# Choosing the buffers of attention probabilities in the kernel's own order account, and inverting layer 1's softmax sums in transposed form

## The chip, the cores and the metric

The kernel runs on one core of one Trainium2 chip. The metric is the device time of one execution in microseconds (us); the time before is the median of three runs. TensorE (PE) multiplies matrices into PSUM, VectorE (DVE) and ScalarE (ACT) work on SBUF and PSUM, GpSimd (POOL) does some elementwise work and issues the DMAs that accumulate, SyncE (SP) issues most others. In the profile PEld is PE's loading of weights, beside its matmuls.

## The reference, cut to what matters

Two layers on x of shape (8, 256, 32, 32), all in float32.

```python
# layer 0: convolutional attention, 8 heads of 32 channels, 1024 queries, 1426 pooled keys
x = x + L0(gn(x))
    # pooled(k_map), pooled(v_map): means at sides 32, 16, 11, 5, each plus a depthwise 3x3 of itself, then layernorm
    attn = softmax(einsum('bhqd,bhkd->bhqk', q_g, k) * SCALE)
    out  = proj(einsum('bhqk,bhkd->bhqd', attn, v) mixed by w_attn)
# layer 1: attention over the 1024 tokens of 256 channels, then 8 experts of three matrices each
t = tokens(x)
t = t + attention(layernorm(t))      # one head of 256
t = t + experts(layernorm(t))        # gate by softmax over the mean of the batch
```

Both softmaxes are computed without a maximum: exponentials, their sums, and a product with the reciprocal of the sum. A guard adds up sums and reciprocals of all softmaxes; should it find them too large, a general version runs behind a branch (it doesn't with these inputs).

## The kernel before, in words

Layer 0's attention is the spine of the first 1916 us. `steps` lists 8 images x 2 groups of four heads (c) x 2 halves of the queries x 11 chunks of 128 keys (the last 18 keys are done once per image, in `tail_scores`). In each step PE computes the scores of one chunk into the only sc buffer (4 PSUM banks, 128 x 2048), ACT takes their Exp into a tile pt (128 x 2048, 1 MB), and PE multiplies the previous step's pt with the values into pv. For the softmax sums, pt tiles are added in pairs: `add` lets an accumulating DMA on POOL's queue add the odd chunk's tile to the even one's; then, in `sums`, DVE adds the pairs 1 to 5 of a unit (b, c, half) to pair 0, and PE multiplies that with ones into a PSUM bank, total. There are six pt buffers. An odd tile is free when its values are multiplied and its DMA has landed, an even one after DVE's addition, that of pair 0 after the product with ones.

`normalise` turns total by 32 x 32 blocks on DVE (each sum stands 32 times, so 16 of 512 columns hold all), inverts 16 numbers, turns them back and multiplies. For the guard, ACT copies total and the reciprocals, 512 elements each, with an accumulator output into a column of `hi` and of `lo`.

Layer 1's attention runs beside it, an image or more behind: `layer1` computes scores and Exp (tiles p1, six buffers), `outputs` adds them up, multiplies with ones, inverts on DVE all 256 sums of a tile that stand in every partition, multiplies with the values and adds the residual. Its guard copies on ACT, of sums and reciprocals, stand before and after the reciprocal and write to the unused half of the same PSUM bank.

The order of every engine's instructions is fixed while the program is built. `Flow` (line 658) keeps an account: `now` for each engine, `ready` and `read` for each tile, with a cost for each operation (`cost`), and 0.15 us or a transfer time (`transfer`) until others see a result. Each piece of work is a generator that yields what it needs next; `step` resumes those that the account calls runnable, by rank, between the steps of the attention: the units have rank 0, layer 1 ranks 5 and 6, depthwise taps 7, expert tiles done ahead 8. `finish` resumes threads until a condition holds, and otherwise picks the one with the earliest start. `note` (line 766) books an instruction and ties it to the one before on its engine, so that every engine keeps the account's order; nearly all instructions are issued there, and so have line 671 in the profile.

`Flow.tile` (line 705) takes the buffer of the tag whose last tile ends first by the account, to book a start time. But which buffer a tile really gets is chosen by the tile framework among those of its tag, and the account doesn't know of uses of a tile that are not yet booked.

From about 1950 us on the experts run, three matrix products each for 8 experts and 16 tiles of 512 tokens, mostly as Strassen products with 7 instead of 8 partial products; a few tiles are done ahead during attention (`experts_ahead`, in the plain form).

Of the kernel before, what the change touches and what calls it, by code (L numbers as in the profile page):

```python
# [8 lines left out]
F32 = mybir.dt.float32  # L9
# [7 lines left out]
P = 128  # L17
C = 256
# [16 lines left out]
MARGIN = 1.5  # L35
AHEAD = {"DVE": 4.0, "ACT": 2.0, "POOL": 1.0, "SP": 10.0}
NEAR = {"DVE": 1.5, "ACT": 2.0, "POOL": 1.0, "SP": 10.0}
BUFS = {"sm": 2, "sx": 1}
AHEAD3 = 3
PACE2 = 8.0  # L40
# [13 lines left out]
class Kit:  # L54
# [3 lines left out]
        self.nc = nc  # L58
        self.n = 0

    def tile(self, pool, shape, tag, bufs=None):
        self.n += 1
        return pool.tile(shape, F32, tag=tag, name=f"{tag}_{self.n}", bufs=bufs)

    def rstd(self, out, var, eps):
# [592 lines left out]
class Flow:  # L658
# [27 lines left out]
    def __init__(self, tc, kit):  # L686
        nc = tc.nc
        self.tc, self.kit = tc, kit
        self.now = dict.fromkeys(("PE", "DVE", "ACT", "POOL", "SP"), 0.0)
        self.last = {}  # L690
        self.ready, self.read, self.writer, self.reader, self.slots, self.open = {}, {}, {}, {}, {}, set()
        self.pe = self.Engine(self, "PE", nc.tensor)
        self.ve = self.Engine(self, "DVE", nc.vector)
        self.act = self.Engine(self, "ACT", nc.scalar)
        self.pool = self.Engine(self, "POOL", nc.gpsimd)
        self.sp = self.Engine(self, "SP", nc.sync)
        self.threads = []
        self.cut = {}
        self.also = {}
        self.tiled = None  # L700
        self.columns = False
        self.left, self.served = [0.0, 0.0], 0.0
        self.credit, self.port = [0.0, 0.0], 0.0

    def tile(self, pool, shape, tag, bufs=1):
        t = self.kit.tile(pool, shape, tag, bufs=bufs)
        slots = self.slots.setdefault(tag, [None] * bufs)
        i = min(range(bufs), key=lambda i: self.end(slots[i]))
        self.ready[t.name] = self.end(slots[i])
        slots[i] = t.name  # L710
        if tag in BUFS:
            self.open.add(t.name)
        return t

    def end(self, name):

# [49 lines left out]
    def note(self, engine, op, ins, args, kwargs):  # L766
# [35 lines left out]
        if "dma" in op:  # L802
            both = out.space == DRAM and srcs[0].space == DRAM
            size = 4e-3 * out.shape[0] * out.free_size() if out.space != DRAM else 4e-3 * srcs[0].shape[0] * srcs[0].free_size()
            lag = self.transfer(engine, end, size * (0.0054 if engine == "POOL" or both else 0.003))
        for n in {*outs, self.key(out)}:
            self.ready[n] = max(self.ready.get(n, 0.0), end + lag)
            self.writer[n] = "DMA" if "dma" in op else engine
# [5 lines left out]
    def transfer(self, queue, at, work):  # L814

        span = max(0.0, at - self.served)
        self.served = max(self.served, at)
        mine, other = queue == "POOL", queue != "POOL"
        left = self.left
        both = 2 * min(left)  # L820
        done = min(span, both) / 2
        for i in range(2):
            left[i] = max(0.0, left[i] - done - max(0.0, span - both))
        left[mine] += work
        return 1.7 + left[mine] + min(left[mine], left[other]) + self.served - at

    @staticmethod
    def key(a):
# [85 lines left out]
def attention(tc, kit, f, outer, ended, nb, consts, x, t1, t2, hn, bounds, vecs, q_t, kv_t, proj_t, gqk_t, wqk, wqkv, vecs1, w1_d, w1c, gate_d, wrc, vecs2, bnvec, w2_d, h2d, between, pre, held):  # L914
# [6 lines left out]
    with ExitStack() as ctx:  # L921
# [39 lines left out]
        nc.scalar.dma_start(pjw, proj_t.rearrange("(k p) f -> p k f", p=P))  # L961
        con = kit.con
        ident, grp = kit.ident, con[:, K_GRP : K_GRP + P]
        heads = T(l1, [P, P + DH], "res", bufs=2)
        nc.scalar.dma_start(heads, consts[:, K_HEAD:K_SEL])
        head = heads[:, :P]
# [26 lines left out]
        def mix():  # L993
# [46 lines left out]
            yield act(wa)  # L1040
            f.act.activation(wa, wa, AF.Exp)
            yield ve(wa)
            rs = T(wp, [P, 2], "wars")
            f.ve.tensor_reduce(rs, wa, AX.X, ALU.add)
            f.ve.reciprocal(rs, rs)
# [18 lines left out]
            for c in range(2):  # L1064
                f.pe.matmul(
                    ps[:, c * C : (c + 1) * C], lhsT=bdt[:, c, :], rhs=pjw[:, c, :], start=True, stop=True
                )
            yield ve(ps)
            raw = T(l1, [P, 2, C], "s")
            f.ve.tensor_copy(raw, ps.rearrange("p (c q) -> p c q", c=2))  # L1070
            for c in range(2):
# [106 lines left out]
            return dy, dx, max(0, -dy), n - max(0, dy), max(0, -dx), n - max(0, dx)  # L1178


        pmaps = [T(pool_, [P, NK], f"p{i}") for i, pool_ in enumerate((between, work))]
        for t in pmaps:
            f.split(t, 512, HW)
        first, large, whole, pooled, asked, halved = {}, [], [], [], [], []
# [67 lines left out]
        def first_keys(half):  # L1252

            n = SIDES[0]
            middle, rest = first["diag"]
            for m in range(2):
                p, acc = first[m]
                pin = p[:, : n * n].rearrange("p (h w) -> p h w", h=n)
                yield pe(p[:, : n * n], middle, rest, tag="sm")
                ps = small()  # L1260
                pout = ps.rearrange("p (h w) -> p h w", w=n)
                for i, tap in enumerate((4, 0, 1, 2, 3, 5, 6, 7, 8)):
                    dy, dx, y0, y1, x0, x1 = windows(tap, n)
                    y0, y1 = max(y0, 16 * half), min(y1, 16 * half + 16)
                    f.pe.matmul(
                        pout[:, y0 - 16 * half : y1 - 16 * half, x0:x1],
                        lhsT=rest[:, 8 * m + i - 1, :] if i else middle[:, m, :],
                        rhs=pin[:, y0 + dy : y1 + dy, x0 + dx : x1 + dx],
                        start=i == 0,
                        stop=i == 8,  # L1270
                    )
                f.act.activation(acc[:, half * 512 : half * 512 + 512], ps, AF.Identity, bias=db(m, 0))
            large.append(("keys", half))

        def taps(c, s, p, acc, base=0):
# [324 lines left out]
        def sums(n, pairs):  # L1600

            for i in range(1, NKC // 2):
                yield until(lambda: len(pairs) > i)
                for j in range(0, 4, 2):
                    s = pairs[0][:, j : j + 2, :]
                    yield ve(s, pairs[i])
                    f.ve.tensor_tensor(s, s, pairs[i][:, j : j + 2, :], ALU.add)
            yield until(lambda: normalised[0] == n)
            yield pe(pairs[0], tag="sm")
            total = small()  # L1610
            for j in range(4):
                f.pe.matmul(
                    total[DH * j : DH * j + DH, :], lhsT=kit.ones[:, :DH], rhs=pairs[0][:, j, :], start=True, stop=True
                )
            return total

        def normalise(b, c, sl, total, n):
# [2 lines left out]
            turned = rec.rearrange("p (j i) -> p j i", i=DH)  # L1620
            yield ve(total)
            f.ve.transpose(rec, total)
            f.act.activation(total, total, AF.Copy, accum_out=hi[:, column[n] : column[n] + 1])
            one = T(work, [P, 16, 1], "one")
            f.ve.reciprocal(one, turned[:, :, 0:1])
            f.ve.transpose(turned, one.to_broadcast([P, 16, DH]))
            f.ve.tensor_tensor(att, att, rec, ALU.mult)
            yield act(rec)
            f.act.activation(rec, rec, AF.Copy, accum_out=lo[:, column[n] : column[n] + 1])

        def project(b):
            if b == nb - 1:
                last = T(work, [P, 2, HW], "pt", bufs=6)
                f.sp.dma_start(last, x[b].rearrange("(k p) n -> p k n", p=P))
            for m in range(2):
# [17 lines left out]
                        f.pool.dma_start(out=t1[b][:, m, sl], in_=xt, accum_op=ALU.add)  # L1653
            if b == nb - 1:
                f.sp.dma_start(t1[b], last)
            projected[0] += 1

        def scale_tokens(src, n):
# [90 lines left out]
        def outputs():  # L1749

            for i in range(4 * nb):
# [13 lines left out]
                ps = small()  # L1765
                f.pe.matmul(ps[:, :C], lhsT=kit.ones, rhs=s[:, 0, :], start=True, stop=True)
                yield ve(ps)
                rec = T(l1, [P, C], "rec1")
                n = 8 * (i // 4) + 4 + i % 4
                f.act.activation(ps[:, C:], ps[:, :C], AF.Copy, accum_out=hi[:, n : n + 1])  # L1770
                f.ve.reciprocal(rec, ps[:, :C])
                f.act.activation(ps[:, C:], rec, AF.Copy, accum_out=lo[:, n : n + 1])
                yield pe(*p1, v, tag="sm")
                ps = small()
                for m in range(2):
                    for kc in range(8):
# [7 lines left out]
                            stop=kc == 7,  # L1784
                        )
                taken[0] += 1
                yield ve(ps, rec)
                m2 = ps.rearrange("p (m q) -> p m q", m=2)
                f.ve.tensor_tensor(m2, m2, rec[:, None, :].to_broadcast([P, 2, C]), ALU.mult)
# [1 line left out]
                    f.ve.scalar_tensor_tensor(res[:, m, :], m2[:, m, :], gb[:, m : m + 1], res[:, m, :], ALU.add, ALU.add)  # L1791
                f.sp.dma_start(t2[b][:, :, q], res)
                f.spawn(norm(b, q, res), 5)

        scaled = [0]

# [24 lines left out]
        def weights1():  # L1821
# [76 lines left out]
            wrs = T(wp, [P, 2, NE], "wrs")  # L1898
            yield from centred(cm, wr, NE, wrs)
            f.sp.dma_start(wrc, wrs)  # L1900
            ready.append(True)

        gw, wv = (T(l1, [P, 2, C], tag) for tag in ("gw", "wv"))
# [4 lines left out]
        def experts_ahead():  # L1908

            yield until(lambda: made[0] == nb and key_parts[0] == 3 * nb)  # L1910
            for e, tag in enumerate(("p0", "kt")):
                w = held["w"][e] = T(between, [P, 2, 2, C], tag)
                f.sp.dma_start(w[:, 0], w1c[:, e])
                f.sp.dma_start(w[:, 1], w2_d[:, e])
# [48 lines left out]
        def unit(b, c, sl, n, pairs):  # L1963
            total = yield from sums(n, pairs)
            yield from normalise(b, c, sl, total, n)
            normalised[0] += 1
            if c and sl.start:
                f.spawn(project(b), 1)

        atts = {}  # L1970
        f.spawn(chain(*map(keys_and_values, range(nb))), 2)
# [21 lines left out]
        for i in range(len(steps) + 1):  # L1993
            if i < len(steps):
# [12 lines left out]
                if kc == NKC - 1:  # L2007
                    f.finish(lambda: key_parts[0] > 3 * b + 2 and (b, 1) in qs and (b or len(asked) == 4))
                    tail_scores(b)
                else:  # L2010
                    pts[i] = scores(b, c, sl, kc)
                f.step()
            if i and steps[i - 1][3] < NKC - 1:
# [7 lines left out]
                f.finish(lambda: kc1 // 4 in vts[b1])  # L2021
                values(b1, c1, kc1, pts[i - 1], pv)
                if kc1 % 2:
                    add(kc1, pts.pop(i - 1), pts[i - 2])
                    pairs.append(pts.pop(i - 2))
                if kc1 == NKC - 2:
# [725 lines left out]
```

## Time and profile before

| | |
|---|---|
| median of 3 runs | 3259.01 us (3258.67 to 3266.59) |
| the profiled execution's own time | 3261.05 us |
| its span, first to last instruction | 3259.2 us |
| PE busy | 3056.5 us (94%) |
| DVE busy | 2406.7 us (74%) |
| ACT busy | 1682.6 us (52%) |
| POOL busy | 1240.7 us (38%) |
| granted PE clock, mean | 0.98 |
| accumulating DMAs pt to pt | 160 of 1 MB, 7.7 us from issue to landing in the median |

The profile has one execution. Its page gives for each engine a row of 40 digits, tenths of busy time in equal slices of the span; PEclk is the share of its full clock that PE was granted. Waits are listed as engine, what it was about to write, and after the arrow what ended its idle time. A row of the order of instructions has start and duration in us, engine, line, operation, the written tile, the read ones, shapes and count, and in brackets the idle time before it.

### The profile page before, as it was taken

What the parts mean: (1) busy time and instruction counts of PE and PEld (TensorE: products, weight loads), DVE (VectorE), ACT (ScalarE), POOL (GpSimd) and SP (SyncE); (2) the same over time, 40 slices, a digit from 0 to 9 for tenths busy, and PEclk for the clock granted to TensorE, in tenths of its full rate; (3) what the DMA queues carried; (4) which work ended last, traced back from release to release, by engine and by line L of the source; (5) the groups of instructions that cost most, each with busy time, mean ns of one, the idle gap of its engine ahead of it and who ended that gap; (6) DMA issues with size and microseconds to landing.
All of it is one profiled execution on the core that took longest, in us unless ns stands there. A gap on an engine that the chain in (4) does not pass through costs nothing.

```text
span 3259.2 us, 55911 instructions
## 1 busy us (share of the span) xinstructions
PE 3056.5 (94%) x22330; PEld 1789.3 (55%) x22330; DVE 2406.7 (74%) x4117; ACT 1682.6 (52%) x2301; POOL 1240.7 (38%) x1327
## 2 busy tenths in 40 slices
PE   8778799999979989989999999999999999999998
PEld 4322234334325334424333356777888888888887
DVE  5886786987877888969754544447888887777776
ACT  4566566666645657657665533333333334444443
POOL 3211413224222232232121112007655667777776
PEclk9899999999989999989999999999999999999999
DMA  1376657665664565565676645225444430000000
GB/s 54 86 153 156 125 124 155 137 148 111 141 145 84 128 151 113 137 143 111 141 182 126 144 111 207 94 88 171 146 149 149 149 117 20 20 20 33 20 14 21
DMA packets 115710, 368.68 MB, mean 113 GB/s; under 512 B 14305, under 2 KB 40233, under 8 KB 92209
## 3 DMA queue, kind: packets, MB, share of 16 engines
q0 software_dynamic: 28608, 179.85, 28.5%
q1 hardware_dynamic: 83472, 183.19, 16.7%
q8 instruction: 178, 2.92, 0.4%
q10 hardware_dynamic: 3360, 1.97, 0.2%
q14 instruction: 92, 0.75, 0.1%
HBM read 116.12 MB, written 83.40 MB: 61 GB/s over the span
## 4 chain that ended last, share of the span: by engine, by line
PE 49%; DVE 6%; DMA 3%; issue 2%; ACT 2%; POOL 1%; SPq 0%; DVEq 0%; POOLq 0%; ACTq 0%
PE bank L671 20%; PE y L671 10%; PE sm L671 9%; PE sx L671 4%; PE sc L671 3%; PE pv L671 3%; DVE h L671 2%; DMA pt<-pt 2%; ACT pt L671 1%; DVE acc L671 1%; DVE u L671 1%; DVE c L671 1%; DVE pt L671 1%; DVE t L671 0%; DMA t<-res 0%
## 5 line engine op out<-in xcount | busy, mean ns | idle before, releaser
L671 ACT ACTIVATE pt<-sc 128x2048 f32<-128x2048 f32 x352 | 660.9, 1877 | 296.7 <-PE sc L671 204.3
L671 DVE SCALAR_TENSOR_TENSOR acc<-p,vec,acc 128x961 f32<-128x961 f32 (+3 forms) x960 | 562.2, 594 | 35.1 <-ACT acc L671 9.4
L671 PE MATMUL sc<-q,kn 32*128 32x512 f32 (+1 forms) x3072 | 428.5, 662 | 125.1 <-ACT pt L671 121.8
L671 DVE TENSOR_TENSOR pt<-pt,pt 128x1024 f32<-128x1024 f32 x320 | 391.9, 1271 | 148.3 <-DMA pt<-pt 123.7
L671 PE MATMUL pv<-pt,vt 128*32 128x512 f32 x2816 | 390.9, 628 | 1.7 <-ACT vt L671 1.2
L671 ACT ACTIVATE h<-h,bnvec 128x512 f32<-128x512 f32 x450 | 340.4, 805 | 61.8 <-DVE h L671 53.1
L671 ACT ACTIVATE p1c<-bank 128x256 f32<-128x256 f32 x225 | 86.2, 383 | 553.5 <-PE bank L671 553.2
L671 POOL TENSOR_TENSOR rstd<-rstd,mhalf 128x4 f32<-128x4 f32 (+2 forms) x88 | 106.6, 1211 | 651.6 <-DVE rstd L671 560.2
L671 POOL DMA_DIRECT2D pt<-pt x160 | 146.3, 916 | 465.4 <-ACT pt L671 376.7
L671 DVE TENSOR_TENSOR h<-p1c,bank 128x512 f32<-128x512 f32 x225 | 153.3, 682 | 200.2 <-PE bank L671 196.5
L671 PEld LDWEIGHTS sc<-q,kn 32*128 32x128 f32 (+1 forms) x3072 | 115.7, 182 | 324.4 <-ACT pt L671 223.2
L671 POOL TENSOR_TENSOR tm<-h,tm 128x256 f32<-128x256 f32 x208 | 239.2, 1150 | 16.3
L671 DVE TENSOR_TENSOR h<-u,bank 128x256 f32<-128x256 f32 x450 | 229.2, 550 | 7.7
L671 PEld LDWEIGHTS pv<-pt,vt 128*32 128x32 f32 x2816 | 56.3, 109 | 281.3 <-issue 262.1
L671 POOL TENSOR_TENSOR tm<-h 128x512 f32<-128x512 f32 x104 | 133.2, 1281 | 202.6 <-ACT h L671 198.5
L671 DVE TENSOR_TENSOR h<-h,gate 128x1024 f32<-128x1024 f32 x128 | 199.9, 1561 | 0.5 <-ACT h L671 0.5
L671 PE MATMUL y<-t,s3e 128*128 128x256 f32 x768 | 187.0, 379 | 3.1 <-POOL t L671 1.7
L671 PE MATMUL bank<-t,s1e 128*128 128x256 f32 x726 | 178.1, 381 | 2.6 <-DVE t L671 2.4
L671 POOL TENSOR_TENSOR t<-h,t 128x256 f32<-128x256 f32 x214 | 169.5, 792 | 16.8
L671 POOL TENSOR_TENSOR t<-h 128x512 f32<-128x512 f32 x107 | 136.1, 1272 | 98.1 <-DVE h L671 77.4
L671 DVE TENSOR_TENSOR u<-h,bank 128x512 f32<-128x512 f32 x225 | 154.7, 688 | 24.7 <-PE bank L671 1.4
L671 PEld LDWEIGHTS y<-t,s3e 128*128 128x128 f32 x768 | 145.7, 190 | 24.0 <-POOL t L671 2.5
(376 smaller groups left out, 5557.5 us busy)
## 6 DMA issues: line engine op xcount, KB each, us to landing
pt<-pt POOLq DMA_DIRECT2D x160, 1024.0 KB, 7.7
h<-h SPq DMA_DIRECT2D x123, 512.0 KB
xi<-in_x_dram SPq DMA_DIRECT2D x16, 512.0 KB
t<-t SPq DMA_DIRECT2D x8, 1024.0 KB
res<-t SPq DMA_DIRECT2D x32, 256.0 KB
t<-res SPq DMA_DIRECT2D x32, 256.0 KB
hn<-res SPq DMA_DIRECT2D x32, 256.0 KB
hn<-hn SPq DMA_DIRECT2D x16, 512.0 KB
```

The costliest lines, as they stand in the source:

```text
L671: ins = fn(*args, **kwargs)
```

## The change

It does three things.

1. The tiles of tags pt and p1 are held from their allocation until `drop` is called after their last booked use. `Flow.tile` takes, among the buffers that aren't held, the one that ends first by the account, and gives each buffer a tag of its own (pt.0 to pt.5), so the framework has no choice left. Ahead of every `scores`, and of the last projection's load, the program waits (`finish`, `until`) in the account until a buffer is vacant: until a tile has been dropped. Two other tiles are renamed (p0, p1 to map0, map1).
2. The account's figure for a DMA that POOL issues goes from 0.0054 to 0.0036 us per KB, and the fixed part of every transfer from 1.7 to 2.2 us.
3. Layer 1's sums are turned by blocks, inverted as 8 numbers, and turned back. The guard's inputs are the numbers and their reciprocals side by side in one small tile (32 in layer 0, 16 in layer 1), which ACT reads once with an accumulator output, at the end of the unit. In layer 0 `normalised` and the spawning of `project` move from `unit` into `normalise`, ahead of that read. A constant of 128 x 32 is loaded on ACT's queue at the start; nothing reads it.

```diff
+OWN = {"pt", "p1"}
@@ Kit.tile
-    def tile(self, pool, shape, tag, bufs=None):
+    def tile(self, pool, shape, tag, bufs=None, slot=None):
         self.n += 1
+        if slot is not None:
+            return pool.tile(shape, F32, tag=f"{tag}.{slot}", name=f"{tag}_{self.n}", bufs=1)
@@ Flow.tile
-        t = self.kit.tile(pool, shape, tag, bufs=bufs)
         slots = self.slots.setdefault(tag, [None] * bufs)
-        i = min(range(bufs), key=lambda i: self.end(slots[i]))
+        own = tag in OWN
+        i = min((i for i in range(bufs) if slots[i] not in self.held), key=lambda i: self.end(slots[i]))
+        t = self.kit.tile(pool, shape, tag, bufs=bufs, slot=i if own else None)
+        if own:
+            self.held.add(t.name)
...
+    def drop(self, *tiles):
+
+        self.held.difference_update(map(self.key, tiles))
+
+    def vacant(self, tag):
+        return any(name not in self.held for name in self.slots.get(tag, [None]))
@@ Flow.note, Flow.transfer
-            lag = self.transfer(engine, end, size * (0.0054 if engine == "POOL" or both else 0.003))
+            lag = self.transfer(engine, end, size * (0.0036 if engine == "POOL" else 0.0054 if both else 0.003))
...
-        return 1.7 + left[mine] + min(left[mine], left[other]) + self.served - at
+        return 2.2 + left[mine] + min(left[mine], left[other]) + self.served - at
@@ attention
+        i32 = T(l1, [P, DH], "i32")
+        nc.scalar.dma_start(i32, consts[:, K_I32:K_SEL])
@@ sums
                     f.ve.tensor_tensor(s, s, pairs[i][:, j : j + 2, :], ALU.add)
+                f.drop(pairs[i])
...
+            f.drop(pairs[0])
             return total
@@ normalise
             f.ve.transpose(rec, total)
-            f.act.activation(total, total, AF.Copy, accum_out=hi[:, column[n] : column[n] + 1])
-            one = T(work, [P, 16, 1], "one")
-            f.ve.reciprocal(one, turned[:, :, 0:1])
-            f.ve.transpose(turned, one.to_broadcast([P, 16, DH]))
+            two = T(work, [P, 32, 1], "two", bufs=2)
+            f.ve.tensor_copy(two[:, :16], turned[:, :, 0:1])
+            f.ve.reciprocal(two[:, 16:], turned[:, :, 0:1])
+            f.ve.transpose(turned, two[:, 16:].to_broadcast([P, 16, DH]))
             f.ve.tensor_tensor(att, att, rec, ALU.mult)
-            yield act(rec)
-            f.act.activation(rec, rec, AF.Copy, accum_out=lo[:, column[n] : column[n] + 1])
+            normalised[0] += 1
+            if c and sl.start:
+                f.spawn(project(b), 1)
+            yield act(two)
+            f.act.activation(T(work, [P, 32, 1], "bin"), two, AF.Copy, accum_out=hi[:, column[n] : column[n] + 1])
@@ project
             if b == nb - 1:
+                yield until(lambda: f.vacant("pt"))
                 last = T(work, [P, 2, HW], "pt", bufs=6)
@@ outputs
+                parts = T(l1, [P, 8, DH], "turn1")
+                f.ve.transpose(parts.rearrange("p j i -> p (j i)"), ps[:, :C])
                 rec = T(l1, [P, C], "rec1")
-                n = 8 * (i // 4) + 4 + i % 4
-                f.act.activation(ps[:, C:], ps[:, :C], AF.Copy, accum_out=hi[:, n : n + 1])
-                f.ve.reciprocal(rec, ps[:, :C])
-                f.act.activation(ps[:, C:], rec, AF.Copy, accum_out=lo[:, n : n + 1])
+                two = T(l1, [P, 16, 1], "two1")
+                f.ve.tensor_copy(two[:, :8], parts[:, :, 0:1])
+                f.ve.reciprocal(two[:, 8:], parts[:, :, 0:1])
+                f.ve.transpose(rec.rearrange("p (j i) -> p j i", i=DH), two[:, 8:].to_broadcast([P, 8, DH]))
...
+                f.drop(*p1)
...
                 f.spawn(norm(b, q, res), 5)
+                n = 8 * (i // 4) + 4 + i % 4
+                yield act(two)
+                f.act.activation(T(l1, [P, 16, 1], "bin1"), two, AF.Copy, accum_out=lo[:, n : n + 1])
@@ the steps
                 else:
+                    f.finish(lambda: f.vacant("pt"))
                     pts[i] = scores(b, c, sl, kc)
...
                 if kc1 % 2:
+                    f.drop(pts[i - 1])
                     add(kc1, pts.pop(i - 1), pts[i - 2])
```

More of the change, by code (lines that the diff above doesn't have):

```diff
@@ L697, in __init__ @@
         self.threads = []
+        self.held = set()
         self.cut = {}
@@ L1042, in mix @@
             yield ve(wa)
+            f.drop(wk)
             rs = T(wp, [P, 2], "wars")
@@ L1068, in mix @@
             yield ve(ps)
+            f.drop(wa, pjw)
             raw = T(l1, [P, 2, C], "s")
@@ L1178, in windows @@
             return dy, dx, max(0, -dy), n - max(0, dy), max(0, -dx), n - max(0, dx)
-        pmaps = [T(pool_, [P, NK], f"p{i}") for i, pool_ in enumerate((between, work))]
+        pmaps = [T(pool_, [P, NK], f"map{i}") for i, pool_ in enumerate((between, work))]
         for t in pmaps:
@@ L1272, in first_keys @@
                 f.act.activation(acc[:, half * 512 : half * 512 + 512], ps, AF.Identity, bias=db(m, 0))
+                if ("keys", 1 - half) in large:
+                    f.drop(p)
             large.append(("keys", half))
@@ L1655, in project @@
                 f.sp.dma_start(t1[b], last)
+                f.drop(last)
             projected[0] += 1
@@ L1900, in weights1 @@
             f.sp.dma_start(wrc, wrs)
+            f.drop(wvr, cm, g)
             ready.append(True)
@@ L1910, in experts_ahead @@
             yield until(lambda: made[0] == nb and key_parts[0] == 3 * nb)
-            for e, tag in enumerate(("p0", "kt")):
+            for e, tag in enumerate(("map0", "kt")):
                 w = held["w"][e] = T(between, [P, 2, 2, C], tag)
@@ L1965, in unit @@
             yield from normalise(b, c, sl, total, n)
-            normalised[0] += 1
-            if c and sl.start:
-                f.spawn(project(b), 1)
         atts = {}
```

## The prediction

> **What bounds the kernel now.** I read the page's slices first, then busy time by stage, then who waited for whom on each engine between 400 and 1950 us, then the order of instructions around single gaps. All durations are of the profiled execution: span 3259.2 us, its time 3261.05 us, that is 2.0 us above the median of the runs (3259.01 us).
>
> ```profile
> PE   8778799999979989989999999999999999999998
> ```
>
> ```profile
> core 0: us, PE busy (x) PEld busy (x) DVE busy (x) ACT busy (x) POOL busy (x), PEclk, DMA share, GB/s
> ...
> 300.00:400.00 100.00, 78.62 (x612) 23.41 (x612) 69.89 (x118) 59.54 (x72) 33.64 (x39) 0.88 0.59 122
> 400.00:600.00 200.00, 192.09 (x2018) 76.66 (x2017) 161.70 (x309) 134.06 (x171) 56.41 (x68) 1.00 0.63 133
> ...
> 800.00:1000.00 200.00, 171.29 (x1639) 70.03 (x1632) 165.82 (x302) 111.64 (x133) 52.85 (x59) 0.96 0.59 129
> ...
> 1400.00:1600.00 200.00, 186.26 (x1704) 71.87 (x1704) 164.82 (x310) 130.64 (x165) 58.66 (x70) 0.94 0.58 120
> ...
> 1950.00:3259.20 1309.20, 1285.50 (x5730) 1079.62 (x5728) 947.60 (x1387) 486.16 (x805) 739.08 (x746) 1.00 0.26 88
> ```
>
> TensorE (PE) bounds it nearly everywhere: 98% busy from 1950 us on, where the change touches next to nothing. Layer 1's work and the experts' work started ahead fill PE whenever layer 0's attention leaves it free, and what isn't done there is done after it. So PE's work is a constant, and only its idle time and its reduced clock can change: 95.7 us idle of the 1550 between 400 and 1950, and 21.4 between 300 and 400. The clock column lacks some 30 us of full speed in 400 to 1950 (0.04 x 200 in 800 to 1000, 0.06 x 200 in 1400 to 1600, and two more rows) and 12 in 300 to 400.
>
> ```profile
> PE sc L671 <- ACT pt L671: 81.7, 65, 6.2
> ...
> ACT sm L671 <- DVE rec L671: 69.6, 34, 4.0
> ...
> ACT pt L671 <- DMA pt<-pt: 57.1, 17, 7.3
> ACT sx L671 <- DVE rec L671: 28.2, 14, 5.3
> ...
> DVE pt L671 <- DMA pt<-pt: 118.1, 42, 14.9
> DVE rec L671 <- ACT sm L671: 24.2, 12, 4.9
> DVE rec L671 <- ACT sx L671: 20.0, 5, 10.5
> ```
>
> Total us, times, longest. PE's idle time is the scores (sc) waiting for the Exp (pt) that empties the one sc buffer. The Exp in turn waits 57.1 us for an accumulating DMA that holds the pt slot it was given, and ScalarE (ACT), which works in order, stands 97.8 us before its guard copies, behind VectorE's (DVE's) transposes and reciprocals.
>
> ```profile
> 932.69 1.88 ACT L671 ACTIVATE pt<-sc 128x2048 f32<-128x2048 f32 x1 [6.83 <-DMA pt<-pt]
> ...
> 934.62 2.09 PE L671 MATMUL sc<-q,kn 32*128 32x512 f32 x8 [5.99 <-ACT pt L671]
> 936.64 1.68 PE L671 MATMUL pv<-pt,vt 128*32 128x512 f32 x8
> 938.71 1.14 PE L671 MATMUL sc<-q,kn 32*128 32x512 f32 x8 [0.39 <-ACT pt L671]
> ```
>
> One such gap: Exp waits 6.83 us, PE 5.99, and the scores after it take 2.09 us instead of 1.14.
>
> **Part 1, the slots.** Exps, additions and sums run in a fixed order, so each Exp of the trace can be tied to the values, DMA, DVE addition or sums that releases its tile. Over the trace 25 Exps wait over 0.4 us for a slot, 79.2 us. In ten of them, 19.2 us, fewer than six tiles were alive: another slot was free. In six more another slot came free 0.8 to 4.9 us earlier than the one waited for; at 945.3 us, say, a DMA was waited for 6.6 us while an addition released a tile after 1.6. Together 36.4 us of Exp waiting come from the choice of slot. PE's gaps behind these Exps, less the 1.00 us that such a gap has without a slot wait (the repeated value), sum to 19 us. The clock adds to it. [...] in 1400 to 1600 the clock is 0.94[...], and scores at 1413.97 already take 2.09 us behind gaps of 2.16 and 0.56. I take the row: of the 42 us of missing clock, PE was busy in 0.8, which is 33, and half follows wrong slots: 16. So 19 + 16 = 35 is what a perfect choice gives; bounds 0 and 35. The account that now chooses has its own errors, so I take three quarters: -26.
>
> Where all six tiles were alive, PE lost about 20 us more. There the new wait for a vacant slot, ahead of the scores, first issues other work (additions, PE fillers) until a tile is dropped. Behind it in program order stand the scores, their Exp and all that ACT queues after. It can fill such a gap, or only move it: 0 to -20, I take -6, nearer to moved, since the slots really are full there.
>
> **Part 2, the sums.** Layer 1, 32 units. DVE loses a reciprocal of 256 (1755 ns) and gets two transposes, a copy and a reciprocal.
>
> ```profile
> L671 DVE RECIPROCAL one<-rec x32: 252/253/256, 185.7 to 1915.0; 128x16 f32<-128x16 f32 x32
> L671 DVE STREAM_TRANSPOSE rec<-one x32: 711/711/712, 186.0 to 1915.3; 128x512 f32<-128x512 f32 x32
> ...
> L671 DVE RECIPROCAL rec<-sm x24: 1746/1757/1758, 482.0 to 2142.9; 128x256 f32<-128x256 f32 x24
> ```
>
> From 16 and 256 elements: (1755 - 253)/240 = 6.26 ns an element, so 8 take 0.20 us. A transpose of 256 lies between half of 711 ns and 711: I take 0.42. The copy is near the 4-element additions (0.16). Sum 1.20, or -0.55 a unit, -18 us. [...] Layer 0 gains one copy of 16 in each of 32 units, +5. Net -12 us of DVE busy time.
> ACT: layer 1 loses two activations of 256 with accumulator reads (0.38 + 0.39 + 2 x 0.19), layer 0 two of 512 (0.58 + 0.63 + 2 x 0.19), and each gets one of 16 or 32 elements with a read, 0.27 + 0.19 (nearest row: 0.29 for 146 elements). That is 32 x (0.69 + 1.13) = -58 us of busy time. Neither engine is the bound, so by itself this is worth nothing. What counts is order: ACT no longer stands before DVE's reciprocal (97.8 us), nor DVE before ACT's first copy (44.2 us). PE's gaps that such an ACT wait made (5.49 us at 383.9, ten more of 0.4 to 1.5) come to 7 us beyond the usual 1.00, and 3 of clock; I take -8 (0 to -10). DVE, 82% busy in 400 to 1600, gets 44 idle and 12 busy us back; additions come earlier and slots with them: 0 to -10, I take -5.
> The moved steps: layer 0's unit counts as normalised, and the projection is spawned, before ACT's single guard read; the projection's DMAs on POOL move up by at most the 0.8 us of that read. The guard read comes last, nobody waits for it but a later tile of its tag (two buffers).
>
> **Part 3, the account's DMA figure.** An accumulating MB was 1.7 + 5.66 us after its issue and is 2.2 + 3.77. In the trace it lands 6.03 us after the issue's end at least, 6.87 in the median, and 47 of 160 come behind an earlier one, at some 5.2 us each. So the old figure is 0.5 too long, the new one 0.9 too short, more under a backlog. DVE will take up additions some 1.4 us earlier in its order, and behind an addition that waits stand the depthwise taps, statistics and normalisations in which layer 1 and the next image wait. Price on PE: 0 to +20, I take +7, since DVE has 18% spare.
>
> **The rest.** The extra constant on ACT's queue at the start costs 0.48 us there (the row of its neighbour): ACT's first instruction waits for these issues, +0.5. The last projection's load waits for a vacant slot: it was issued at 1901.8 us for use at 1917.8, so nothing up to some 8 us of delay; if that cover goes, up to 5. SP's other transfers keep their places.
>
> Sum: -26 - 6 - 8 - 5 + 7 + 0.5 = -37.5 us, 3261.05 to 3223.5; against the median, 2.0 lower, 3221.5.
>
> **The rivals.** (B) The account is nearly exact: wrong and full slots both vanish with their clock, and the reciprocal too. Idle time 19 + 20 + 7, clock 33, DVE -5: 84, or 3175; I put it at 3185. For it: layer 1's filler abounds until 1916 us. Against: the account's DMA figure. (C) The slot isn't the cause, or the account picks as badly: DVE's late additions (a tile that an addition frees lives 19.1 us past its Exp in the median, one that a DMA frees 9.6) keep all six full, and the wait merely changes its name. Half of part 2 remains, less part 3: about 3255. (D) Slower: the short DMA figure. 42 additions wait already; 1.4 us more on each and 0.7 on forty more is 87 us of DVE standing still, of 210 us idle in 400 to 1600. [...] a third of it reaching PE is +29, less 13 of part 2: 3275.
>
> **How the numbers follow.** The measurement can tell about 0.3%, 10 us. Likeliest (A) 0.55, 3221.5, own range 3195 to 3245; B 0.20; C 0.14; D 0.11. Faster A + B = 0.75, same C = 0.14, slower D = 0.11. The range goes from under B's 3185 to C's 3255 and its error: 3178 to 3260.
>
> **What would show it.** Right: "ACT pt <- DMA pt<-pt" under 30 us in 400 to 1950, PE's idle time there near 65, the clock at 0.97 or more in each 200 us, "ACT sm/sx <- DVE rec" gone, reciprocals near 0.20 us. Part 3 right: "DVE pt <- DMA pt<-pt" above 118. Wrong: slot waits as before under another releaser (C), DVE's DMA waits above 180 us with PE's idle time up (D), or a changed count of expert tiles done ahead (three now), which alters PE's work.

## The result, and the profile after

The changed kernel takes 3245.08 us in the median (7 runs, 3241.31 to 3253.27); the kernel before, run beside it, 3259.67. The ratio is 0.9954, 95% interval 0.9944 to 0.9964: 14.6 us faster, where 37.5 were forecast.

The profiled execution (3241.31 us, span 3238.0) by stage; columns as before: PE, PE's weight loads, DVE, ACT, POOL busy, granted clock, DMA share, GB/s. First the kernel before:

```profile
400.00:1950.00 1550.00, 1454.29 (x14423) 590.84 (x14422) 1165.27 (x2129) 963.59 (x1185) 390.54 (x444) 0.98 0.62 134
```

The changed kernel; the stage with the lowest granted clock between 400 and 1950 us is in the last row:

```profile
400.00:1950.00 1550.00, 1463.88 (x14978) 588.66 (x14975) 1155.39 (x2223) 926.68 (x1087) 403.84 (x471) 0.98 0.63 140
0.00:400.00 400.00, 318.21 (x2280) 117.76 (x2280) 297.97 (x614) 231.19 (x303) 117.20 (x141) 0.93 0.52 117
...
1400.00:1600.00 200.00, 187.36 (x1834) 71.77 (x1837) 152.60 (x288) 120.36 (x141) 42.01 (x48) 0.96 0.57 120
```

PE's idle time between 400 and 1950 us fell from 95.7 to 86.1 us, not to the 65 foreseen. The waits there, of PE, ACT and DVE (total us, times, longest):

```profile
PE sc L674 <- ACT pt L674: 59.4, 64, 3.1
PE sm L674 <- DVE turn L674: 6.0, 2, 3.9
PE sm L674 <- DVE res L674: 5.3, 3, 3.1
```

```profile
ACT bin L674 <- DVE two L674: 39.8, 20, 6.1
...
ACT pt L674 <- DMA pt<-pt: 13.3, 4, 6.3
```

```profile
DVE pt L674 <- DMA pt<-pt: 204.3, 72, 13.5
```

The slots moved the way that was expected: Exp's waits for a DMA that holds its slot fell from 57.1 to 13.3 us, and PE's longest gap in front of scores from 6.2 to 3.1. Counted as in the prediction, over the whole trace, slot waits over 0.4 us fell from 79.2 to 29.2 us, and the share due to the choice of slot from 36.4 to about 2. Not all of this is the slots' doing: with the two other parts alone Exp's slot waits are already down to 27.2 us (table below). But DVE now stands before its additions for 204.3 us instead of 118.1, and PE's waits for DVE's work of layer 1 have grown: 6.0 us for turn, which is new, and 5.3 for res, 1.0 before.

Where DVE stands matters. Of the 118.1 us before, only 37.8 lay between 400 and 1600 us, where DVE is 82% busy; 80.4 lay after 1600, where it is half idle (busy 175.5 us of 350). In the changed kernel it is 105.2 and 99.2: four fifths of the increase fall where DVE has much to do.

What one such wait does, in DVE's order and then in PE's (start, duration, operation, idle time before it):

```profile
455.22 2.35 DVE L674 TENSOR_TENSOR pt<-pt,pt 128x1024 f32<-128x1024 f32 x2
461.00 2.36 DVE L674 TENSOR_TENSOR pt<-pt,pt 128x1024 f32<-128x1024 f32 x2 [3.43 <-DMA pt<-pt]
463.28 0.44 DVE L674 STREAM_TRANSPOSE turn<-sm 128x256 f32<-128x256 f32 x1
```

```profile
459.14 0.68 PE L674 MATMUL sx<-xl,kvw 128*32 128x146 f32 x16
463.77 2.79 PE L674 MATMUL sm<-p,v 128*32 128x256 f32 x24 [3.95 <-DVE turn L674]
```

DVE stands 3.43 us before an addition whose DMA hasn't landed. Queued behind it is the turning of layer 1's sums, which frees the PSUM bank that PE wants next: PE stands 3.95 us.

The ledger below is worked out from each trace, in us. PE's idle time is span less busy time. The clock records hold only full and half speed: 21 stretches of half speed in the kernel before, with PE busy for 100.6 us of them, and 20 in the changed one, 91.8 us. In the trace of before, a 128x256 product into bank starts 427 ns after the one ahead of it at half speed, and 216 ns at full. So half of the busy time at half clock is counted as the clock's cost, an estimate, and busy time less that cost as the work at full clock.

| kernel | span | PE idle | clock's cost | work at full clock |
|---|---|---|---|---|
| before | 3259.2 | 202.8 | 50.3 | 3006.2 |
| after | 3238.0 | 185.6 | 45.9 | 3006.5 |
| held slots and new sums, old DMA figure | 3207.5 | 154.3 | 43.4 | 3009.8 |
| new DMA figure alone | 3277.7 | 208.4 | 55.8 | 3013.5 |

In all twenty traces of this study the work lies between 3002 and 3015 us, and before and after differ by 0.3 us. That PE's work is nearly a constant held, although the number of expert tiles done ahead, which the prediction had named as a risk, did change: four instead of three here, two to four over all kernels.

### The profile page after: what moved, and what is told of

Same layout as the page of the kernel before. It is cut to its first block, busy times and chain, and to the rows that moved or that the text cites. A ratio compares the mean times of both kernels' runs of the same rounds, so it can differ in the third digit from the quotient of the medians.

```text
span 3238.0 us, 57063 instructions
## 1 busy us (share of the span) xinstructions
PE 3052.4 (94%) x22924; PEld 1774.1 (55%) x22924; DVE 2388.8 (74%) x4234; ACT 1631.2 (50%) x2168; POOL 1224.7 (38%) x1309
## 4 chain that ended last, share of the span: by engine, by line
PE 46%; DVE 3%; issue 2%; DMA 1%; POOL 1%; ACT 1%; DVEq 0%; POOLq 0%; ACTq 0%
PE bank L674 21%; PE y L674 10%; PE sm L674 9%; PE sc L674 2%; PE pv L674 2%; PE sx L674 2%; DVE h L674 1%; DMA pt<-pt 1%; DVE u L674 1%; DVE c L674 1%; ACT pt L674 1%; POOL t L674 0%; DVE t L674 0%; POOL rstd L674 0%; DVE pt L674 0%
## 5 line engine op out<-in xcount | busy, mean ns | idle before, releaser
L674 DVE SCALAR_TENSOR_TENSOR acc<-map,vec,acc 128x961 f32<-128x961 f32 (+3 forms) x960 | 562.3, 594 | 34.6 <-ACT acc L674 9.3
L674 ACT ACTIVATE h<-h,bnvec 128x512 f32<-128x512 f32 x440 | 332.8, 805 | 59.7 <-DVE h L674 50.6
L674 DVE TENSOR_TENSOR h<-u,bank 128x256 f32<-128x256 f32 (+1 forms) x440 | 223.9, 550 | 7.6
L674 PE MATMUL sm<-y,t 128*32 128x256 f32 (+1 forms) x2432 | 198.2, 379 | 1.1 <-DVE res L674 1.0
L674 PE MATMUL sm<-p,v 128*32 128x256 f32 (+1 forms) x2064 | 179.5, 385 | 3.9 <-DVE turn L674 3.9
```

Source lines behind the costliest of these rows:

```text
L674: ins = fn(*args, **kwargs)
```

## The experiments

Theory 1, formed on the result: slots and sums gave what was forecast or more, and the shorter DMA figure took much of it back, since DVE takes up additions too early and stands still. Rivals: (2) the gaps only move, layer 1 can't fill more; (3) only the sums count.

**The three parts, one by one and in pairs.** The parts are switched by these edits of the changed kernel; the old sums are the lines of before in `normalise`, `unit` and `outputs`. The renamed tiles and the extra constant stay in every switched kernel; they weren't tested by themselves.

```diff
# slots off: the framework chooses, nothing is held
-OWN = {"pt", "p1"}
+OWN = set()
# old DMA figure
-size * (0.0036 if engine == "POOL" else 0.0054 if both else 0.003)
+size * (0.0054 if engine == "POOL" or both else 0.003)
-        return 2.2 + left[mine] + ...
+        return 1.7 + left[mine] + ...
```

Held slots and new sums, old figure. 

> The changed kernel with the account's old DMA figure (1.7 us + 0.0054 us per KB). Theory 1 (the short figure took back what the slots gave: DVE takes additions up too early and stands still): DVE's wait for pt<-pt DMAs between 400 and 1950 us falls from 204 to about 120 us, PE's idle time there from 86 to about 70, time near 3230. Theory 2 (the gaps only move, since layer 1 can fill only so much, and the figure is neutral): 3245 within 6 us, PE's idle time there 80 to 90 whatever DVE waits. Theory 3 (the slots do nothing, the sums carry the gain): 3245 as well.

Held slots and new figure, old sums. 

> Slots and new DMA figure, sums as before. Theory 1: sums are worth 5 to 10, so 3250 to 3255, DVE's DMA waits near 200 us. Theory 2: 3247 to 3252. Theory 3: no gain, 3259 within 5.

New figure and new sums, slots by the framework. 

> New figure and new sums, but the tile framework chooses the slots (no tile is held). Theory 1: slot waits of Exp as before (57 us between 400 and 1950) or more, DVE's DMA waits near 200 us, time 3260 to 3270. Theory 2: 3250 to 3258. Theory 3: 3245 within 5.

Held slots alone. 

> Slots alone: old figure, old sums. Theory 1: Exp's slot waits under 20 us between 400 and 1950, DVE's DMA waits near 120, time near 3237. Theory 2: about 3250. Theory 3: 3259 within 5.

New sums alone. 

> The new sums alone: the framework chooses the slots, old DMA figure. Theory 1a (slots and sums add up: 3199.5 against 3235.6 for slots alone is what the sums are worth anywhere): 3220 to 3230. Theory 1b (the sums pay only where the slots are free, since otherwise the Exp waits for its slot whatever ACT does): 3245 to 3255, with Exp's slot waits between 400 and 1950 us still near 57 us.

New figure alone. 

> The new DMA figure alone. Theory 1 (it costs by DVE's early take-up, in any company): DVE's DMA waits rise from 118 to 160 or more, time 3270 to 3295. Rival (it costs only together with the held slots, where the account's times choose the slot): DVE's waits rise as well, but 3260 within 6.

| slots | sums | figure | median us | ratio to before (95%) | DVE waits for pt DMAs, 400 to 1950 | Exp's slot waits there |
|---|---|---|---|---|---|---|
| | | | 3259 to 3261 | 1 | 118.1 | 57.1 |
| x | | | 3235.55 | 0.9922 (0.9909 to 0.9936) | 119.8 | 1.9 |
| | x | | 3224.38 | 0.9893 (0.9877 to 0.9909) | 112.3 | 36.1 |
| | | x | 3279.6 | 1.0063 (1.0049 to 1.0077) | 192.6 | 33.1 |
| x | x | | 3199.5 | 0.9813 (0.9795 to 0.9831) | 135.2 | 20.5 |
| x | | x | 3265.96 | 1.0016 (1.0008 to 1.0024) | 201.6 | 10.1 |
| | x | x | 3255.61 | 0.9988 (0.9979 to 0.9996) | 160.9 | 27.2 |
| x | x | x | 3245.08 | 0.9954 (0.9944 to 0.9964) | 204.3 | 13.3 |

Each part has four pairs that differ in it alone. Slots: -0.78, -0.80, -0.47, -0.34%, mean -0.60% or -19 us. Sums: -1.07, -1.09, -0.75, -0.62%, mean -0.88% or -29 us. Figure: +0.63, +0.94, +0.95, +1.41%, mean +0.98% or +32 us. Their sum is -0.50%, for -0.46 measured. Rivals 2 and 3 fall: without the new figure the other two parts add up to 61 us in this order of the instructions.

Theory 1's times held for slots alone, sums alone (its form 1a) and figure alone. The others were missed: slots and sums came out 30 us below 3230, slots_figure 11 us above its range, and figure_sums 4 us below it, inside that of theory 2, with DVE's waits at 161 us instead of some 200 and Exp's slot waits at 27 instead of 57 or more. In part theory 1 took the sums for too little; in part it is chance, as shown below.

Between slots alone and slots with sums ACT's waits change as foreseen. Slots alone first, ACT and PE between 400 and 1950 us:

```profile
ACT sm L674 <- DVE rec L674: 90.6, 34, 6.1
...
ACT sx L674 <- DVE rec L674: 48.1, 17, 6.9
```

```profile
PE sc L674 <- ACT pt L674: 54.2, 63, 5.0
```

With the sums (old figure):

```profile
ACT bin L674 <- DVE two L674: 27.6, 21, 3.9
```

```profile
PE sc L674 <- ACT pt L674: 40.8, 35, 4.2
```

138.7 us of ACT standing before its guard reads became 27.6, and PE's wait for the Exp fell from 54.2 to 40.8 us.

**Which half of the figure.** Fixed part 2.2 us with the old 0.0054 per KB: 

> The changed kernel with half of the figure: fixed part 2.2 (all transfers), the old 0.0054 per KB. Theory 1 (what costs is that the accumulating DMA is booked too short): here it is booked too long, 7.9 us for a measured 6.9 after the issue, so as with the old figure: 3195 to 3212, DVE's DMA waits 135 us or less. Rival (the fixed part costs, since it reaches every SP transfer too and delays layer 1's loads in the account): 3225 to 3250.

Fixed part 1.7 with the new 0.0036: 

> The other half: fixed part 1.7, new 0.0036 per KB, 5.5 us booked. Theory 1: shorter still than in the changed kernel, so no better than it: 3245 to 3260, DVE's DMA waits 204 us or more. Rival: 3195 to 3215.

Measured: fixed part 3200.49 (0.982, 0.9805 to 0.9835), DVE's waits 122.8 us; per KB 3269.2 (1.0021, 1.0012 to 1.0031), waits 196.3. It is the shorter time per KB, though per_kb came out 9 us slower than expected, with waits slightly under the expected 204; the fixed part, which also reaches SP's loads, costs nothing that shows.

**What the figure does.** It acts in two ways: on when an addition is taken up (what the DMA writes is booked ready), and on when a slot is booked free (what it reads). Each was shortened by itself, with held slots, new sums and the old figure:

```diff
+        short = 2.0 if "dma" in op and engine == "POOL" else 0.0
         for n in {*outs, self.key(out)}:
-            self.ready[n] = max(self.ready.get(n, 0.0), end + lag)
+            self.ready[n] = max(self.ready.get(n, 0.0), end + lag - short)
```

> Held slots, new sums, old DMA figure (3199.5), but what an accumulating DMA writes is booked 2.0 us earlier; what it reads stays booked as before. So only DVE's additions are taken up earlier. Theory 1 (this is how the new figure costs): DVE's DMA waits between 400 and 1950 us about 200 us, time 3240 to 3265. Rival (the figure costs because slots, which the DMA's source releases, are booked free too early): as without it, 3195 to 3212.

The mirror image has `- short` in the line that books `self.read`. 

> The mirror image: only what the accumulating DMA reads, the slot it releases, is booked 2.0 us earlier. Theory 1: 3195 to 3215, DVE's DMA waits near 135. Rival: 3240 to 3265.

The third keeps the changed kernel's figure and holds back the taking up alone, in `sums`:

```diff
+                    yield until(lambda: f.now["PE"] + 1.5 >= f.ready[f.key(pairs[i])] + 1.9)
                     yield ve(s, pairs[i])
```

> The changed kernel with its new figure, but an addition may be taken up only 1.9 us later by the account's PE time than the figure would allow. Theory 1: the loss comes back, 3200 to 3220, DVE's DMA waits 140 us or less. Rival: 3240 to 3250.

Measured: early_addition 3268.82 (1.0031, 1.0022 to 1.0039), early_slot 3229.12 (0.9905, 0.9886 to 0.9925), late_addition 3197.68 (0.9815, 0.9795 to 0.9834). DVE between 400 and 1950 us, early_addition and then late_addition:

```profile
DVE pt L674 <- DMA pt<-pt: 190.9, 58, 12.3
```

```profile
DVE pt L674 <- DMA pt<-pt: 136.4, 43, 10.2
```

PE's first waits in the same stretch, in the same order:

```profile
PE sc L674 <- ACT pt L674: 56.8, 57, 3.4
PE sx L674 <- ACT kt L674: 8.2, 1, 8.2
PE sx L674 <- DMA t<-t: 4.4, 1, 4.4
PE sm L674 <- ACT acc L674: 4.3, 2, 3.2
PE sm L674 <- DVE st L674: 4.3, 1, 4.3
```

```profile
PE sc L674 <- ACT pt L674: 35.9, 38, 3.2
PE sm L674 <- DVE res L674: 9.8, 5, 3.6
```

Early booking of what the DMAs write brings the loss (4 us above the expected range), and late additions undo it under the new figure (2 us under the range). The first edit also books the 28 accumulating DMAs of the projection early, beside those of the additions; the last touches the additions alone, so it is the one that ties the loss to them. early_slot was 14 us above its theory's bounds; that needed the next test.

**Chance of the order.** Any shift of the account reorders all engines, so kernels that mean the same differ. Four kernels shift a fixed part by 0.05 us, and one early_slot by 0.6.

> Held slots, new sums, old per-KB figure, fixed part 1.65 instead of 1.7: a reordering without meaning. If order by chance moves little: 3199.5 within 6. If the differences seen so far are partly chance: more than 10 away from 3199.5.

> The same with 1.75: 3199.5 within 6, or, if order by chance matters, more than 10 away.

> As early_slot, but the slot is booked free 1.4 us early instead of 2.0. If early booking of slots costs by itself: between 3199.5 and 3229, near 3220. If early_slot's loss was a chance of its order: 3195 to 3208.

> The changed kernel with 2.15 instead of 2.2 us: a reordering without meaning. If the short figure costs 30 to 50 us whatever the order: 3235 to 3275, DVE's DMA waits between 400 and 1950 us at 180 us or more. If the loss was a chance of one order: 3195 to 3230.

> The same with 2.25: 3235 to 3275 with DVE's DMA waits at 180 us or more, or, if it was chance, 3195 to 3230.

| | shifted down | as it is | shifted up |
|---|---|---|---|
| old figure (1.65, 1.7, 1.75), us | 3225.53 | 3199.5 | 3218.7 |
| DVE's DMA waits | 136.3 | 135.2 | 167.8 |
| new figure (2.15, 2.2, 2.25), us | 3259.1 | 3245.08 | 3233.34 |
| DVE's DMA waits | 183.5 | 204.3 | 178.2 |

Either row spans 26 us. So two single kernels that differ by less than that prove nothing about an edit. early_slot_14 took 3200.88 us, as its expectation for chance had it; with early_slot the mean is 3215, that of the old figure's row, so nothing shows that slots booked free early cost anything. The 61 us above are a lucky draw too: the mean of the old figure's row is some 45 us below the time before.

The figure's cost stands: 3245.8 against 3214.6 in the means of the rows, 31 us, and the rows don't overlap. It stands more firmly over all thirteen kernels with held slots and both halves of the new sums. The five that take additions up early (the new figure's row, per_kb, early_addition) need 3233 to 3269 us, the eight others 3198 to 3229. DVE's waits tell the two kinds apart, but they don't rank the kernels within a row: 167.8 us go with 3218.7 and 136.3 with 3225.5.

fixed_225 lies 2 us under the expected range, with DVE's waits 2 us under theirs. The shifted fixed_215 is as slow as before (0.9995, 0.9989 to 1.0002): how much of the changed kernel's own 14.6 us is luck of its order can't be told. A part's mean over four pairs is uncertain by some 9 us, an estimate: a standard deviation of about 13 us for a kernel, as in the two rows, gives 18 for a difference and half of that for the mean of four. So the figure's 32 us and the sums' 29 are over three times their uncertainty; the slots' 19 is only twice, and the least sure of the three.

**The sums by halves, and later additions.** Layer 0's half alone, with held slots and the old figure (`outputs` as before): 

> Held slots, old figure, and only layer 0's half of the new sums (one guard read of 32 elements); layer 1 inverts and reads as before. Between slots alone (3235.6) and slots with both halves (3199.5). Theory P (layer 1's half carries the gain: DVE's 1.755 us reciprocal and the turn-taking of DVE and ACT on one bank): 3228 to 3238. Theory Q (layer 0's half does: ACT's two reads of 512 elements, behind DVE's transposes): 3198 to 3208. If both do alike: about 3217.

Measured 3215.75 (0.9865, 0.9843 to 0.9887): halfway, 20 us for layer 0's half and 16 for layer 1's, within the chance of orders. In this trace ACT still waits 58.5 us behind DVE's rec and DVE's rec 36.4 behind ACT, both in layer 1.

The additions later still, 2.6 for 1.9 in the line above: 

> As late_addition (3197.7), the additions taken up 2.6 us later than the new figure would allow instead of 1.9. If DVE's standing still is all that costs: 3190 to 3198, DVE's DMA waits under 120 us. If tiles held longer then cost more: above 3203, with longer slot waits of Exp.

Measured 3202.72 (0.9824, 0.981 to 0.9839), DVE's DMA waits 108.7 us, Exp's slot waits 26.8 instead of 20.9. It can't be told from late_addition. The versions at 3198 to 3203 us (held slots and new sums, with the old figure, with 2.2 + 0.0054, or with late additions) beat both kernels, the changed one by 1.3% or more (3202.7 / 3245.1 = 0.987); of that, an order shifted by 0.05 us can take back up to 26 us.

## Why the prediction was right or wrong

The sign and most mechanisms were right. The step that failed is the price of part 3, which rested on a wrong reason; parts 1 and 2 were probably mis-sized too, in opposite directions. Each of the three measured worths below is uncertain by some 9 us.

- **That PE's work is fixed** and only idle time and clock count: right, 3002 to 3015 us in every trace.
- **Part 1, the slots**, -26 and -6: probably too large. On the time it was -19 (-11 to -26 in the four pairs). The choice of slot cost 36.4 us of Exp's waits in the one trace that the prediction had. Counted the same way, the three other kernels in which the framework chooses have 11 to 14 us, and those with held slots 0 to 12. So the trace of before was a bad draw, and its 36.4 us were taken for the rule.
- **The clock in part 1**, 16, rested on the author's estimate that half of the missing clock follows wrong slots; how near that was can't be told. The clock's cost fell by 4.4 us in the changed kernel and by 6.7 with slots alone, but it moves as much with the order: 31 to 45 us in the kernels with held slots and no early additions, and 31.5 with the new sums alone, without held slots (50.3 before). What brings half clock isn't shown either: nine stretches of it begin between 400 and 1950 us in the changed kernel; two follow gaps of 3.95 and 3.58 us, and in the 8 us ahead of the seven others no gap of PE is over 3.2 us (the longest in each, 1.19 to 3.12).
- **Part 2, the sums**, -8 and -5: the durations held, and the worth was about twice as large, -29 (-20 to -36). The new instructions of layer 1, in the changed kernel:

```profile
L674 DVE COPY two<-turn x32: 170/172/789, 463.8 to 2140.9; 128x8 f32<-128x8 f32 x32
L674 DVE RECIPROCAL two<-turn x32: 191/196/200, 463.8 to 2141.0; 128x8 f32<-128x8 f32 x32
L674 DVE STREAM_TRANSPOSE turn<-sm x24: 434/444/450, 463.3 to 2140.4; 128x256 f32<-128x256 f32 x24
```

  With the second transpose (0.45) they take 1.26 us (1.20 forecast) where the reciprocal of 256 took 1.755. ACT's read takes 0.218 us (0.27 forecast). DVE's busy time fell by 18 us (12 forecast), ACT's by 51 (58). The weak step was to price ACT's 98 us of waits only by the PE gaps that one could see behind them (7 us). What the runs show in its place is -29 us for the part. The likely reason, argued and not shown, is that an Exp that comes earlier also empties sc and frees what is queued behind it; which of ACT's order and DVE's time brings more wasn't separated.
- **Part 3, the figure**, "0 to +20, I take +7, since DVE has 18% spare": this step failed. It was +32 (+20 to +46). Spare time of DVE was no cover: what is queued behind a waiting addition is what PE then waits for, as at 461 us in the trace above, and additions held back bring the loss down again (3197.7 us with the new figure). Rival D had this mechanism, and a price near the measured one, +29. Its 87 us of added standing, for 86.2 measured, are luck in part: it put 1.4 us on each of 42 waits and 0.7 on forty more, and what came was 30 more waits of the same mean length, 2.8 us. Half of the 42 lay after 1600 us, outside the stretch for which it reckoned.
- **The rest**, +0.5: the constant's issue took 0.48 us as foreseen, and ACT's first instruction begins 0.3 us later. The last projection's load is issued 7 us before its use instead of 16, and nothing waits for it.
- **The signs named in advance**: Exp's slot waits under 30 us (13.3), DVE's DMA waits above 118 (204.3), reciprocals near 0.20: right. "ACT sm/sx <- DVE rec" is gone by name, but ACT waits 39.8 us for the numbers it reads instead. PE's idle time near 65 and a clock of 0.97 in every stage: wrong (86.1, and 0.96 in 1400 to 1600). DVE's waits above 180 marked D, with PE's idle time up: against the old figure it is up, by 31 us (185.6 for 154.3 over the whole span).

So -37.5 should have been -19 - 29 + 32 = -16, for -14.6 measured. Parts 1 and 2 together, -45 forecast and -48 measured, agree by luck, since their errors cancel; the figure's 25 us are what is left.

## What to carry to other kernels

In an order fixed in advance, price a booked duration that is too short by what stands queued behind the instruction that then waits, not by the engine's average spare time; against the measured median of 6.9 us, too long by 0.5 to 1.0 us cost nothing that shows here, too short by 0.9 cost 1%. Split a change that does several things before believing its total: here two parts worth some 48 us hid a third that took two thirds of it back. And shift a constant that means nothing before you read anything into a few tenths of a per cent: here 0.05 us of it moved the time by up to 26 us.

## What was unexpected of the hardware

An accumulating DMA of 1 MB from SBUF to SBUF lands 6.03 us after its issue ends at least in the kernel before and 6.04 in the changed one; in the median 6.9 in both. When an earlier DMA that POOL issued has not landed as its issue ends, it lands 4.3 us after that one at least and 5.8 in the median (61 cases in the changed kernel). DVE's float32 reciprocal costs 0.20 us for 8 elements a partition, 0.25 for 16 and 1.755 for 256, four times a transpose of the same 256 (0.444).
